# A recommender's 1,600 gather steps: the loop laid out straight, and the row weights summed into PSUM

## The chip, the cores and the metric

The kernel runs on one core of a Trainium2 chip. The metric is the device time in microseconds (us), the median of several runs. A separate execution with the hardware profiler on gives the profile; its own time is shown beside the median, because the two are not equal here.

The engines of a core are named as in the profile: PE multiplies matrices (PEld is its weight load), DVE does elementwise work and reductions, ACT activation functions, POOL (GpSimd) here issues the indirect DMAs, SP issues plain ones.

## The reference

16,384 samples, each with a history of 200 items, an item, a user and a category. Embeddings have 64 columns. What is computed, cut to what matters:

```python
def dice(x, alpha, axis):
    mean = jnp.mean(x, axis=axis, keepdims=True)
    var = jnp.var(x, axis=axis, keepdims=True)
    p = jax.nn.sigmoid((x - mean) * jax.lax.rsqrt(var + EPS))
    return x * (p + alpha * (1.0 - p))

u, it, c = u_emb[user], i_emb[item], c_emb[cate]
h = i_emb[hist]                                   # 200 x 16384 x 64
itb = jnp.broadcast_to(it[None], h.shape)
feat = jnp.concatenate([h, itb, h - itb, h * itb], axis=-1)
a = dice(feat @ au_W1 + au_b1, au_alpha, axis=1)  # 36 columns, moments over the samples
w = a @ au_W2 + au_b2                             # one weight for a history row
cur = jnp.sum(w * jax.lax.stop_gradient(h), axis=0)
z = jnp.concatenate([u, it, c, cur], axis=-1)
z = dice(z @ W1 + b1, alpha1, axis=0)
z = dice(z @ W2 + b2, alpha2, axis=0)
return z @ W3 + b3
```

Nearly all the time is in the lines from `h` to `cur`.

## The kernel before

**Prologue.** The kernel first multiplies the whole item table by the part of `au_W1` that acts on h alone, and writes a table in DRAM (`table`) whose rows are 128 numbers: the embedding (64) and this product (64 with padding). The part that depends on the item alone is written to `xi`, in 8 pieces. Users, items and categories are gathered and laid out for the head (`uicT`).

**Steps.** The history is worked off in 1,600 steps: 200 history positions (`l`) by 8 pieces (`ND`) of 2,048 samples, 16 on each of 128 partitions (`TD`). Step k does, written out in this order by `step` (from line 462), the work of several steps at once, so that a step's work is spread over eleven:

- `fetch(k)`: 16 indirect DMAs on POOL (line 213 in `gather`), each for 128 rows of 512 bytes from `table` into one of 12 `land` buffers, by indices in `idx` (SBUF); and the piece of `xi`, on SP's queue.
- `turn(k-1)`, DVE: line 390 transposes the embeddings from `land` into PSUM (`ph`); line 391 multiplies them by the item (`itT`) into `hx`; line 392 transposes the second half of the rows.
- `product(k-1)`, PE (line 244): `hx` times `blk_m` onto what ACT has put into `px` (line 476, `preload`).
- `hidden(k-2)`, DVE: line 397 adds both halves and puts the sum back into `land`; line 399 takes its statistics.
- `gates(k-10)`, ACT: lines 405 and 410, the sigmoid and its scale and shift, into `pg` (PSUM).
- `weigh(k-10)`, DVE: line 417 multiplies gate and value in `pg`; line 418 transposes back into `land`; line 420 sums each row to its weight `r`; line 425 multiplies the embedding rows by r plus a bias, into `pg`; line 429 adds that to `cur`.
- In one step of eight, `moments`: the mean and variance of a history position, some fifteen small DVE instructions and a square root on ACT (lines 436 to 460).

Here `ph` and `pg` are PSUM tiles, `px` are two PSUM tiles, and `r` is a small SBUF tile with two buffers. In the steps `ph` is written and read by DVE alone.

**Order and queues.** Each engine works through its own list in the order of the code; `tc.manual_schedule()` keeps the order as written. Semaphores carry the dependencies: a gather waits for the last use of its `land` buffer and for the gather eight places before it; line 390 waits for all 16 gathers of its step.

**The loop.** Of the 200 history positions, `rest_l` = 200 % 24 + 24 = 32 are laid out straight at the end (256 steps). The 168 before run in a hardware loop, `tc.For_i`, of 7 passes with 24 positions (192 steps) each. The body is straight code. The indices of the next position are loaded by `fetch_ids` in every eighth step, at an address that depends on the loop's register:

```python
        rest_l = L % LPB + LPB
        with tc.For_i(0, L - rest_l, LPB) as l0:
            with tc.manual_schedule():
                for k in range(LPB * ND):
                    fetch_ids(k, l0, LPB + 1)
                    step(k)
```

In the straight part `step` gets `last`, by which the final 144 steps (`SPAN`) use one of the `px` tiles only; the other one computes the first layer of the head piece by piece (`base_of_layer1`). After the steps the head follows: two layers with dice and the output.

Of the kernel before, what the change touches and what calls it, by code (L numbers as in the profile page):

```python
# [8 lines left out]
F32 = mybir.dt.float32  # L9
# [5 lines left out]
P = 128  # L15
# [2 lines left out]
CH = 512  # L18
S = 32
CD = 2 * CH  # L20
LPB = 24
LAND = 12
SPAN = 144
EARLY = 4
IDX = 2
# [4 lines left out]
def din_kernel(  # L30
# [25 lines left out]
    L, B = r_hist.shape  # L56
    NT = B // P
    TD = 2 * CD // P
    ND = NT // TD
# [5 lines left out]
    small = ctx.enter_context(tc.tile_pool(name="small", bufs=2))  # L65
# [40 lines left out]
    for a in range(P // S):  # L106
        r = ts(a, S)
# [4 lines left out]
        for q, (a0, n) in enumerate(parts):  # L112
            c, w = slice(a * S, a * S + n), au_w[r, :, :, a0 : a0 + n]
# [3 lines left out]
    for a in range(P // S):  # L117
        for q, (a0, n) in enumerate(parts):
            r, u = slice(a * S, a * S + n), slice(a0, a0 + n)
# [21 lines left out]
    ph = psum.tile([P, CD], F32, name="ph")  # L141
# [78 lines left out]
    def load_hist_ids(i, l):  # L220
        nc.sync.dma_start(idx[i], r_hist[ds(l, 1), :].rearrange("l (p n) -> p (l n)", n=NT))

    def halves(t, n=TD):

        return t.rearrange("p (e n t) -> p e n t", e=2, t=S)[:, :, :n]
# [14 lines left out]
    def first_layer(dst, blk, rhs, n=CH, onto=False):  # L240

        for q in range(2):
            for e in range(2):
                nc.tensor.matmul(  # L244
                    dst[:, q * CH : q * CH + n], blk[:, e, q], rhs[:, e * CH : e * CH + n],
                    start=(e == 0 and not onto), stop=(e == 1), skip_group_check=onto,
                )
# [101 lines left out]
    with ExitStack() as main:  # L349
# [25 lines left out]
        def by_row(t):  # L375
            return t.rearrange("p (n d) -> p n d", d=D)

        def x_of(k):
            return of_rows(land[k % LAND][:, :, D:])

        def fetch(k):
            l, c = divmod(k, ND)
            gather(land[k % LAND], idx[l % IDX][:, ts(c, TD)], table)
            nc.sync.dma_start(xit[k % XI], xi[c])

        def turn(k):

            rows = land[k % LAND]
            hm, hw = hx[k % 2][:, 0], hx[k % 2][:, 1]
            nc.vector.transpose(halves(ph), of_rows(rows[:, :, :D]))  # L390
            nc.vector.tensor_mul(hm, ph, itT[:, k % ND])  # L391
            nc.vector.transpose(halves(hw), of_rows(rows[:, :, D:]))  # L392

        def hidden(k, px):

            l, c = divmod(k, ND)
            nc.vector.tensor_add(x_of(k), halves(px), halves(hx[k % 2][:, 1]))  # L397
            for q in range(2):
                nc.vector.bn_stats(stats[l % 2][:, q, c, :], x_of(k)[:, q])  # L399
# [15 lines left out]
        def weigh(k):  # L415

            nc.vector.tensor_mul(halves(pg), halves(pg), x_of(k))  # L417
            nc.vector.transpose(x_of(k), halves(pg))  # L418
            r = small.tile([P, TD], F32, tag="r", name="r")
            nc.vector.tensor_reduce(  # L420
                r, land[k % LAND][:, :, D:], mybir.AxisListType.X, ALU.add
            )
            c = k % ND
            rows = land[k % LAND][:, :, :D]
            nc.vector.scalar_tensor_tensor(  # L425
                by_row(pg), r.unsqueeze(2).to_broadcast([P, TD, D]), au_bias2, rows,
                ALU.add, ALU.mult,
            )
            nc.vector.tensor_add(cur[:, ts(c, TD)], by_row(pg), cur[:, ts(c, TD)])  # L429
# [32 lines left out]
        def step(k, last=None):  # L462


            def has(j):
                return last is None or j <= last

            def single(j):

                return last is not None and j > last - SPAN  # L470

            def px_of(j):
                return pxs[0 if single(j) else j % 2]

            def preload(j):
                nc.scalar.copy(px_of(j), xit[j % XI])  # L476

            def product(j):
                first_layer(px_of(j), blk_m, hx[j % 2][:, 0], onto=True)

            if has(k):
                fetch(k)
            if has(k - 1):
                turn(k - 1)
                if not single(k - 1):
                    product(k - 1)
            if has(k - 10):
                if k % ND == 2:
                    moments((k - 10) // ND)
                gates(k - 10)  # L490
                weigh(k - 10)
            if has(k - 2):
                hidden(k - 2, px_of(k - 2))
            if has(k - 1) and single(k - 1):
                preload(k - 1)
                product(k - 1)
            if has(k) and not single(k):
                preload(k)

        def fetch_ids(k, l0, n):  # L500
            l, c = divmod(k, ND)
            if c == 0 and l + 1 < n:
                load_hist_ids((l + 1) % IDX, l0 + l + 1)

        def window(j):
            return slice(2 * ZB * (J - 1 - j), 2 * ZB * (J - 1 - j) + P)
# [22 lines left out]
                        yield  # L529
                        yield  # L530

        rest_l = L % LPB + LPB
        with tc.For_i(0, L - rest_l, LPB) as l0:
            with tc.manual_schedule():
                for k in range(LPB * ND):
                    fetch_ids(k, l0, LPB + 1)
                    step(k)


        K = rest_l * ND  # L540

        def home(i):
            t = land[(K + i // 2) % LAND].rearrange("p (s n) d -> p s (n d)", s=2)
            return t[:, i % 2]
# [6 lines left out]
        def rest_of(c):  # L551
            return home(homes[ND + c // J])

        def load_base(*cs):
            for c in cs:
                nc.sync.dma_start(z_of(c), zbase[c])
# [45 lines left out]
        with tc.manual_schedule():  # L602
            work = base_of_layer1()
            for k in range(K):
                fetch_ids(k, L - rest_l, rest_l)
                step(k, last=K - 1)
                if k > K - SPAN:
                    next(work, None)
            load_base(0, 1)
            for k in range(K, K + 10):  # L610
                step(k, last=K - 1)
                if k < K + 4:
                    load_base(*((2, 3), (ND, ND + 1), (4, 5), (6, 7))[k - K])
                c = k - K - 2
                if c >= 1:
                    keep1(c - 1)
                if c >= 0:
                    layer1(c)
            keep1(ND - 1)

            spare = [home(i) for i in range(18, 24)]
            fa, fb = row_factors(0, ZA, P), row_factors(1, ZB, P)
            def activated(c):
                if c % J == 0:
                    dice(rest_of(c), rest_of(c), spare[4 + c // J], fb, zb)
                a = spare[c % 4]
                dice(a, z_of(c), a, fa, za)
                layer(
                    (px, pz, pg, ph)[c % 4][: 2 * Z2], [(w2a, a), (w2b[:, c % J], rest_of(c))]
                )  # L630

            def keep2(c):
                t = home(10 + c)[: 2 * Z2]
                nc.scalar.activation(
                    t, (px, pz, pg, ph)[c % 4][: 2 * Z2], AF.Identity, bias=z2[0]
                )
                row_sums(2, 2 * Z2, c, t)

            for c in range(ND + 2):
                if c < ND:  # L640
                    activated(c)
                if c >= 2:
                    keep2(c - 2)
            f2 = row_factors(2, Z2, 2 * Z2)
            n = ND * 2 * ZO
            for c in range(ND):
                a = spare[c % 4]
                dice(a, home(10 + c)[: 2 * Z2], a, f2, z2)
                at = (ND - 1 - c) * 2 * ZO
                for i in range(2):  # L650
                    nc.tensor.matmul(  # L651
                        px[:n, ts(i, CH)], w3[:, at : at + n], a[: 2 * Z2, ts(i, CH)],
                        start=(c == 0), stop=(c == ND - 1),
                    )

            rT, res = spare[4][:S], spare[5][:S]
            nc.vector.transpose(rT, px[:S])
            rT = rT.rearrange("t (i n c g o) -> t i g c n o", i=2, n=TD, c=ND, g=2)
            for i in range(2):
                for g in range(2):  # L660
                    nc.vector.tensor_add(
                        res[:, ts(2 * i + g, NT * ZO)].rearrange("t (c n o) -> t c n o", c=ND, n=TD),
                        rT[:, i, g],
                        bias3.unsqueeze(1).unsqueeze(1).to_broadcast([S, ND, TD, ZO]),
                    )
            nc.sync.dma_start(
                out.rearrange("(q t n) o -> t q (n o)", t=S, n=NT),
                res.rearrange("t (q m) -> t q m", q=4),
            )
# [30 lines left out]
```

## Time and profile before

| | us |
|---|---|
| median of 3 runs | 36713.39 |
| lowest and highest run | 36705.22, 36721.51 |
| the profiled execution | 32925.16 |
| its span, first to last instruction | 32922.9 |
| first gather of the steps begins at | 488.6 |
| last gather of the steps begins at | 32710.6 |
| DVE idle at line 390, waiting for gathers | 10590.4 |
| ACT idle at line 476, waiting for DVE line 397 | 22124.3 |

The profiled execution is the shorter one, by about a tenth. All durations of single instructions come from it.

A line of the groups reads: source line, engine, operation, what it writes and reads, shape, count; then the busy time in all in us and the mean of one in ns; then the engine's idle time just before these instructions, and what ended it. "issue" means that the engine waited for nothing that the profile shows. A line of the timeline reads: start in us from the start of the span, duration in us, engine, line, operation, operands, count, and in brackets the idle time before it.

### The profile page before, as it was taken

The page shows a single profiled execution, that of the slowest core. Times are in us where ns is not written, and L with a number is a line of the kernel's source. Part 1 is how long each engine was busy: PE and PEld are TensorE (multiplying, and loading weights), DVE is VectorE, ACT ScalarE, POOL GpSimd, SP SyncE. Part 2 cuts the span into 40 slices and gives each one's busy share as a digit, 9 for nine tenths or more (in the row PEclk, how much of TensorE's full clock was granted, in tenths as well). Part 3 has the DMA queues.
Part 4 walks back from the last instruction along what each step waited for, and adds up shares of the span by engine and source line. Part 5 has one row for each costly group of instructions (what it writes and reads, how often), then busy time and mean ns, then how long its engine had stood idle before and what let it go on. Part 6 is the DMA issues. An engine that isn't in the chain of part 4 may idle for free. (4 is left out here: it accounts for less than half of the span.)

```text
span 32922.9 us, 106947 instructions
## 1 busy us (share of the span) xinstructions
PE 9897.1 (30%) x13650; PEld 3847.8 (12%) x13650; DVE 20486.1 (62%) x21482; ACT 7127.0 (22%) x8732; POOL 24717.0 (75%) x25991
## 2 busy tenths in 40 slices
PE   4222222222222222222222222222222222223333
PEld 1111111111111111111111111111111111111111
DVE  5666666666666666666666666666666666666666
ACT  1222222222222222222222222222222222222222
POOL 7777777777777777777777777777777777777775
PEclk7666666666666666666666666666666666666666
DMA  5222222222222222222222222222222222223332
GB/s 161 80 79 78 79 78 79 79 78 78 79 79 79 79 78 79 79 78 78 79 79 79 79 79 78 79 79 78 78 80 79 78 80 78 79 79 88 92 92 66
DMA packets 1219178, 2681.59 MB, mean 81 GB/s; under 512 B 552540, under 2 KB 578684, under 8 KB 1212284
## 3 DMA queue, kind: packets, MB, share of 16 engines
q0 software_dynamic: 831488, 1691.97, 19.6%
q1 hardware_dynamic: 375228, 914.56, 9.0%
q10 hardware_dynamic: 11712, 67.98, 0.5%
q14 instruction: 635, 5.20, 0.1%
q8 instruction: 115, 1.88, 0.0%
HBM read 2599.36 MB, written 73.35 MB: 81 GB/s over the span
## 5 line engine op out<-in xcount | busy, mean ns | idle before, releaser
L213 POOL DMA_INDIRECT land<-table,idx x25600 | 24348.1, 951 | 7875.1 <-issue 7674.0
L244 PE MATMUL px<-hx,blk_m 128*128 128x512 f32 x12824 | 9453.7, 905 | 22727.6 <-DVE hx L391 20633.8
L390 DVE STREAM_TRANSPOSE ph<-land 128x1024 f32<-128x1024 f32 x1601 | 2016.5, 1259 | 10697.6 <-DMA land<-table,idx 10590.4
L244 PEld LDWEIGHTS px<-hx,blk_m 128*128 128x128 f32 x12824 | 3670.8, 301 | 28507.3 <-issue 23397.1
L476 ACT COPY px<-xit 128x1024 f32<-128x1024 f32 x1600 | 1626.6, 1017 | 22124.3 <-DVE land L397 22124.3
L405 ACT ACTIVATE pg<-land,fac 128x512 f32<-128x512 f32 x3220 | 2508.9, 779 | 85.8 <-DVE cur L429 25.0
L417 DVE TENSOR_TENSOR pg<-pg,land 128x1024 f32<-128x1024 f32 x1610 | 1939.0, 1204 | 925.2 <-ACT pg L410 925.0
L410 ACT ACTIVATE pg<-pg,au_al,au_1al 128x512 f32<-128x512 f32 x3220 | 2419.2, 751 | 106.6
L425 DVE SCALAR_TENSOR_TENSOR pg<-r,au_bias,land 128x1024 f32<-128x1024 f32 x1610 | 2085.1, 1295 | 56.7
L399 DVE BATCH_NORM_STATS2 st<-land 128x6 f32<-128x512 f32 x3204 | 2061.9, 685 | 54.3
L418 DVE STREAM_TRANSPOSE land<-pg 128x1024 f32<-128x1024 f32 x1610 | 2011.7, 1250 | 55.4
L429 DVE TENSOR_TENSOR cur<-pg,cur 128x1024 f32<-128x1024 f32 x1610 | 1970.7, 1224 | 55.0
L420 DVE TENSOR_REDUCE r<-land 128x16 f32<-128x1024 f32 x1610 | 1964.0, 1220 | 55.3
L391 DVE TENSOR_TENSOR hx<-ph,itT 128x1024 f32<-128x1024 f32 x1601 | 1960.3, 1224 | 56.2
L392 DVE STREAM_TRANSPOSE hx<-land 128x1024 f32<-128x1024 f32 x1601 | 1975.3, 1234 | 0.0
L397 DVE TENSOR_TENSOR land<-px,hx 128x1024 f32<-128x1024 f32 x1602 | 1945.1, 1214 | 0.0
L455 ACT ACTIVATE std<-var,eps 32x2 f32<-32x2 f32 x201 | 59.2, 295 | 2577.3 <-DVE var L451 2577.3
L405 ACT ACT_TABLE_LOAD x209 | 268.1, 1283 | 297.5 <-DVE fac L460 172.0
L244 PE MATMUL px<-rT,blk_h 128*128 128x512 f32 (+1 forms) x392 | 220.9, 726 | 168.2 <-DVE rT L295 168.2
L455 ACT ACT_TABLE_LOAD x201 | 257.9, 1283 | 3.5
L439 DVE COPY every<-mv 32x4 f32<-32x4 f32 x804 | 161.7, 201 | 15.2
L213 POOL DMA_INDIRECT land<-in_L_rec_i_emb,ids x128 | 126.4, 987 | 41.0 <-issue 38.6
(110 smaller groups left out, 1537.0 us busy)
## 6 DMA issues: line engine op xcount, KB each, us to landing
xit<-xi SPq DMA_DIRECT2D x1601, 512.0 KB
land<-table,idx POOLq DMA_INDIRECT x25600
table<-tab ACTq DMA_DIRECT2D x48, 1024.0 KB
tab<-in_L_rec_i_emb SPq DMA_DIRECT2D x48, 512.0 KB
zt<-uicT SPq DMA_DIRECT2D x48, 512.0 KB
idx<-in_r_hist SPq DMA_DIRECT2D x200, 64.0 KB
uicT<-t ACTq DMA_DIRECT2D x24, 512.0 KB
zbase<-zt SPq DMA_DIRECT2D x10, 512.0 KB
```

The lines of the kernel that those rows point to most:

```text
L213: nc.gpsimd.indirect_dma_start(out=dst[:, n, :], out_offset=None, in_=rows, in_offset=bass.IndirectOffsetOnAxis(ap=ids[:, n : n + 1], axis=0),
L244: nc.tensor.matmul(dst[:, q * CH : q * CH + n], blk[:, e, q], rhs[:, e * CH : e * CH + n], start=(e == 0 and not onto), stop=(e == 1), ski ...
L390: nc.vector.transpose(halves(ph), of_rows(rows[:, :, :D]))
L391: nc.vector.tensor_mul(hm, ph, itT[:, k % ND])
L392: nc.vector.transpose(halves(hw), of_rows(rows[:, :, D:]))
L399: nc.vector.bn_stats(stats[l % 2][:, q, c, :], x_of(k)[:, q])
L405: nc.scalar.activation(halves(pg)[:, q], x_of(k)[:, q], AF.Sigmoid, bias=facs[i][:, 1, q : q + 1], scale=facs[i][:, 0, q : q + 1],)
L410: nc.scalar.activation(pg[:, ts(q, CH)], pg[:, ts(q, CH)], AF.Identity, bias=au_al[:, q : q + 1], scale=au_1al[:, q : q + 1],)
L418: nc.vector.transpose(x_of(k), halves(pg))
L420: nc.vector.tensor_reduce(r, land[k % LAND][:, :, D:], mybir.AxisListType.X, ALU.add)
L425: nc.vector.scalar_tensor_tensor(by_row(pg), r.unsqueeze(2).to_broadcast([P, TD, D]), au_bias2, rows, ALU.add, ALU.mult,)
L429: nc.vector.tensor_add(cur[:, ts(c, TD)], by_row(pg), cur[:, ts(c, TD)])
```

## The change

Three things: the hardware loop goes, and all 200 history positions are laid out straight in the part that was the tail; `fetch_ids` loses the loop's register; and `r`, the weights of the rows, is no longer a tile in SBUF, but the first 16 columns of the PSUM tile `ph`. The lines after it are moved up by one, by eight after the loop: what was line 425 is line 424.

```diff
-LPB = 24
@@ weigh
             nc.vector.tensor_mul(halves(pg), halves(pg), x_of(k))
             nc.vector.transpose(x_of(k), halves(pg))
-            r = small.tile([P, TD], F32, tag="r", name="r")
+            r = ph[:, :TD]
             nc.vector.tensor_reduce(
                 r, land[k % LAND][:, :, D:], mybir.AxisListType.X, ALU.add
             )
@@
-        def fetch_ids(k, l0, n):
+        def fetch_ids(k):
             l, c = divmod(k, ND)
-            if c == 0 and l + 1 < n:
-                load_hist_ids((l + 1) % IDX, l0 + l + 1)
+            if c == 0 and l + 1 < L:
+                load_hist_ids((l + 1) % IDX, l + 1)
@@
-        rest_l = L % LPB + LPB
-        with tc.For_i(0, L - rest_l, LPB) as l0:
-            with tc.manual_schedule():
-                for k in range(LPB * ND):
-                    fetch_ids(k, l0, LPB + 1)
-                    step(k)
-
-
-        K = rest_l * ND
+
+        K = L * ND
@@ the steps and the head
             for k in range(K):
-                fetch_ids(k, L - rest_l, rest_l)
+                fetch_ids(k)
                 step(k, last=K - 1)
```

## The prediction

> **What bounds the kernel now.** I read the page's head and busy shares first, then its costliest groups, then a stretch of the timeline inside a pass of the loop, and last a stretch across one of the loop's turns. Busy shares and groups:
>
> ```profile
> span 32922.9 us, 106947 instructions
> PE 9897.1 (30%) x13650; PEld 3847.8 (12%) x13650; DVE 20486.1 (62%) x21482; ACT 7127.0 (22%) x8732; POOL 24717.0 (75%) x25991
> L213 POOL DMA_INDIRECT land<-table,idx x25600 | 24348.1, 951 | 7875.1 <-issue 7674.0
> L390 DVE STREAM_TRANSPOSE ph<-land 128x1024 f32<-128x1024 f32 x1601 | 2016.5, 1259 | 10697.6 <-DMA land<-table,idx 10590.4
> L425 DVE SCALAR_TENSOR_TENSOR pg<-r,au_bias,land 128x1024 f32<-128x1024 f32 x1610 | 2085.1, 1295 | 56.7
> ```
>
> POOL is 75% busy, but its 25,600 gathers with the idle time between them make 24,348.1 + 7,875.1 = 32,223 us, and that idle time is "issue": POOL waits for nobody. The first gather starts at 488.6 us. With what follows the last one that is the whole span. DVE, the next engine, waits 10,590 us for gathers at L390, some 6.6 us in each of 1,600 steps. So the end is set by the pace at which POOL issues gathers, and a change is worth what it does to that pace.
>
> The pace is even. This is DVE beside POOL in an ordinary step:
>
> ```profile
> 15024.31 1.22 DVE L420 TENSOR_REDUCE r<-land 128x16 f32<-128x1024 f32 x1
> 15024.33 0.94 POOL L213 DMA_INDIRECT land<-table,idx  x1 [0.31 <-issue]
> ...
> 15025.56 1.29 DVE L425 SCALAR_TENSOR_TENSOR pg<-r,au_bias,land 128x1024 f32<-128x1024 f32 x1
> 15025.58 0.95 POOL L213 DMA_INDIRECT land<-table,idx  x1 [0.30 <-issue]
> ...
> 15026.83 0.94 POOL L213 DMA_INDIRECT land<-table,idx  x1 [0.30 <-issue]
> ```
>
> A gather takes 0.94 us, the pause 0.30, the period is 1.249 us. And this is the first step after a turn of the loop:
>
> ```profile
> 15959.49 0.94 POOL L213 DMA_INDIRECT land<-table,idx  x1 [0.30 <-issue]
> 15970.05 1.28 ACT L405 ACT_TABLE_LOAD   x1 [15.81 <-PEq L533]
> 15970.10 1.26 DVE L390 STREAM_TRANSPOSE ph<-land 128x1024 f32<-128x1024 f32 x1 [15.59 <-PEq L533]
> ...
> 15971.12 0.94 POOL L213 DMA_INDIRECT land<-table,idx  x1 [10.69 <-issue]
> ...
> 15978.35 1.29 DVE L425 SCALAR_TENSOR_TENSOR pg<-r,au_bias,land 128x1024 f32<-128x1024 f32 x1
> 15978.61 1.84 POOL L213 DMA_INDIRECT land<-table,idx  x1 [0.30 <-issue]
> 15979.68 1.22 DVE L429 TENSOR_TENSOR cur<-pg,cur 128x1024 f32<-128x1024 f32 x1
> ```
>
> Two things are to be seen. At the turn (L533) all engines stop and POOL idles 10.69 us where it idles 0.30. And the gather that begins 0.26 us after the start of L425 takes 1.84 us, not 0.94. In the ordinary step L425 began within 20 ns of a gather, so that the next one came 1.27 us later and lost nothing. L425 is the one DVE instruction of a step that reads two large operands from SBUF (r and the rows in land); L391, L397, L417 and L429 have one of theirs in PSUM. Over the trace, gathers that begin 200 to 400 ns after L425 take 1.80 us in the mean (200 of them), 600 to 800 ns after it 1.37 us, 800 to 1,000 ns after it 1.22 us; those that begin under any other DVE line, at any distance, take 0.94. The held gather always ends about 2.1 us after L425's start: it resumes some 1.16 us after that start. So L425 holds a gather for up to about 1.04 us (the longest gather is 1,981 ns, against a median of 944), and what a step loses depends on the phase of L425 against the gathers.
>
> [...] a gather reads its indices from idx in SBUF, and is held under L425 alone, by up to 1.04 us. [...]
>
> **The change part by part.** The profiled execution took 32,925.16 us, 2 us over its span; the median of the runs is 36,713.39, so 3,788 us more, 148 ns for each of 25,600 gathers. No view tells where these lie. I make the sum on the profiled execution first and then ask what carries over.
>
> *The loop goes.* 1,344 of 1,600 steps stood in 7 passes of 192. POOL's pauses at the turns: 7.42 us after the first pass, 10.69 each after the next five, 3.32 at the exit; less 0.30 each that is 62 us. All of it is POOL's time, hence on the path. The instructions of a step and their waits stay as they are, and so do both halves of the ring (192 is a multiple of 12 land buffers and of 2 index buffers). SP issues the same 200 index loads, now from constant addresses; they have a whole row of 8 steps, 160 us, to land. Does straight code cost POOL more? The last 256 steps were straight already: there the mean period is 1.256 us, as in the passes. I take nothing; an open bound is below.
>
> *r moves to ph.* L420 writes 128x16 to PSUM, L425 reads it from there. [...] ph is free then: L390 fills it and L391 empties it earlier in the same step on the same engine, so no wait is added, and PE does not touch ph in the steps. [...]
>
> L425 then has one SBUF input and should hold no gather. In the profiled execution that gives back 25,600 × (951.1 − 944) ns = 182 us; some 200 of the held gathers are those of the one step in eight that runs the moments, where DVE comes about a microsecond late against POOL, as after a turn.
>
> Sum for the profiled execution: 62 + 182 = 244 us of 32,925, or 0.7%. What is late next is still POOL, at 25,600 × 1.249.
>
> *What carries over.* The loss at L425 hangs on a phase that 35 ns decide: the ordinary step runs free only because L425's start falls on a gather's start. In the runs without a profile a gather's period is another: 36,713 − 489 − 211 (the prologue and the tail) = 36,013 us over 25,600, or 1.407 us in the mean if POOL's pace carries it all. The chain from the last landing to L425 (some 8 us) then falls elsewhere in the period. Bounds for a step's loss: nothing, if the phase is lucky, and 1.04 us, so 0 to 1,664 us in all. With no reason for any one phase I take the mean over a period of 1.407: a gather is held in 1.04/1.407 = 74% of phases, by 0.52 us on average, 0.385 us a step, 616 us in all. With 62 us for the loop: 36,713 − 678 = 36,035.
>
> **The rivals.** *The phase in the runs is the profile's.* For it: the phase follows from DVE lengths near the gather's period, which hold in both. Against: the runs are 11% slower, so some length differs. 36,713 − 244 = 36,469.
>
> *Nothing measurable comes of it.* If the runs' phase is lucky in all steps, the loop's 62 us alone are left: 36,651, within 0.2% (73 us, about what a measurement of this kernel can tell from no change).
>
> *The unexplained 3,788 us belong to the loop form or to L425 in a way that the profile does not show.* Without them: 32,925 − 244 = 32,681. For it: held gathers are the only loss on POOL that hangs on timing. Against: one L425 in a step can hold one gather, 1.04 us, and the excess is 2.37 us a step.
>
> *Slower: straight code feeds POOL more slowly than the loop.* [...] the runs have an excess whose place is unknown. Its place would be the pause of 0.30 us before each of the 21,504 gathers that were in the loop. It decides from 678/21,504 = 32 ns each (11 ns against the profile's 244). At 5% of 1.407 us, 70 ns, it costs 1,505 us: 36,713 − 244 + 1,505 = 37,974. Against it: the equal periods in the straight part of the profile[...].
>
> **How the numbers follow.** Uniform phase 0.45; the profile's phase 0.28; nothing measurable 0.10; the large gain 0.05; slower 0.12. The forecast is that of the first, 36,035. Its own range is 34,990 (1,664 + 62 gained) to 36,640. Widened to 34,980 to 36,700 it takes in the first three cases, some 0.83. Faster by over 0.2%: 0.45 + 0.28 + 0.05 = 0.78; the same 0.10; slower 0.12.
>
> **What would show it.** In the profile after: the longest gather of the steps near 950 ns, not 1,981, and their mean duration at 944; no pause of POOL above a few us once the first steps are through; gathers' busy and idle time together near 31,980 us; the span near 32,680; L424 (today's L425) still 1.29 us. If gathers are still held near 1.8 us, the two-input reading is wrong. If the gather's period is above 1.26 us, straight code has a price. If the runs gain far more or less than the profile, the phase, or the unexplained excess, decided.

## The result, and the profile after

| | before, us | after, us | ratio, 95% interval |
|---|---|---|---|
| first comparison, 12 runs each | 36717.45 | 36711.88 | 0.9998, 0.999 to 1.0006 |
| predicted | | 36035 | 0.9815 |

The change does nothing that can be measured. These are the lines of the page of the kernel after that answer to those shown of before:

```profile
span 36719.1 us, 106470 instructions
PE 9930.6 (27%) x13650; PEld 3856.1 (11%) x13650; DVE 20623.6 (56%) x21482; ACT 7114.3 (19%) x8725; POOL 27140.0 (74%) x25991
L212 POOL DMA_INDIRECT land<-table,idx x25600 | 26771.0, 1046 | 9142.2 <-issue 8927.5
L396 DVE TENSOR_TENSOR land<-px,hx 128x1024 f32<-128x1024 f32 x1602 | 1959.8, 1223 | 8263.6 <-remote 5280.2
L389 DVE STREAM_TRANSPOSE ph<-land 128x1024 f32<-128x1024 f32 x1601 | 2012.6, 1257 | 5571.7 <-DMA land<-table,idx 5298.4
L424 DVE SCALAR_TENSOR_TENSOR pg<-ph,au_bias,land 128x1024 f32<-128x1024 f32 x1610 | 2081.7, 1293 | 57.2
```

This profile has the span of the timed runs; that of before had been 10% shorter. The gathers with their pauses make 26,771.0 + 9,142.2 = 35,913 us, 1.403 us for each, where the first profile had 32,223 us and 1.259. A gather's mean is 1,046 ns, not the 944 of the forecast, although L424 no longer reads two operands from SBUF. New is a wait of DVE at L396, 5,280 us in all, for PE's semaphore ("remote": its release has no record); the wait for gathers at L389 is smaller by about the same.

The timeline of the kernel after shows how the gathers come to that mean. It is 15 us in the middle of the run:

```profile
15002.42 1.12 POOL L212 DMA_INDIRECT land<-table,idx  x1 [0.30 <-issue]
...
15003.84 0.94 POOL L212 DMA_INDIRECT land<-table,idx  x1 [0.30 <-issue]
15003.98 1.29 DVE L424 SCALAR_TENSOR_TENSOR pg<-ph,au_bias,land 128x1024 f32<-128x1024 f32 x1
...
15005.09 0.94 POOL L212 DMA_INDIRECT land<-table,idx  x1 [0.30 <-issue]
...
15013.83 0.94 POOL L212 DMA_INDIRECT land<-table,idx  x1 [0.30 <-issue]
...
15015.60 1.93 POOL L212 DMA_INDIRECT land<-table,idx  x1 [0.83 <-issue]
...
15017.84 1.13 POOL L212 DMA_INDIRECT land<-table,idx  x1 [0.30 <-issue]
...
15019.27 1.09 POOL L212 DMA_INDIRECT land<-table,idx  x1 [0.31 <-issue]
```

From 15,003.84 to 15,013.83 there are eight periods of 1.249 us: POOL's own pace, as in the first profile. L424 holds nothing here: over the whole trace gathers that begin 200 to 400 ns after it take 0.99 us in the mean (179 of them, my count), where L425 had made them 1.80. Then a gather takes 1.93 us after a pause of 0.83, and the next ones come some 1.4 us apart. POOL runs ahead, is held, and runs ahead again. Counted over the whole trace, 16 gathers take 22.43 us in the mean, 1.402 us each.

### The profile page after: what moved, and what is told of

The parts are those of the page before. It is cut to its first block, busy times and chain, and to the rows that moved or that the text cites. A ratio compares the mean times of both kernels' runs of the same rounds, so it can differ in the third digit from the quotient of the medians.

```text
span 36719.1 us, 106470 instructions
## 1 busy us (share of the span) xinstructions
PE 9930.6 (27%) x13650; PEld 3856.1 (11%) x13650; DVE 20623.6 (56%) x21482; ACT 7114.3 (19%) x8725; POOL 27140.0 (74%) x25991
## 3 DMA queue, kind: packets, MB, share of 16 engines
q0 software_dynamic: 831488, 1691.97, 17.8%
q8 instruction: 112, 1.84, 0.0%
## 5 line engine op out<-in xcount | busy, mean ns | idle before, releaser
L212 POOL DMA_INDIRECT land<-table,idx x25600 | 26771.0, 1046 | 9142.2 <-issue 8927.5
L396 DVE TENSOR_TENSOR land<-px,hx 128x1024 f32<-128x1024 f32 x1602 | 1959.8, 1223 | 8263.6 <-remote 5280.2
L389 DVE STREAM_TRANSPOSE ph<-land 128x1024 f32<-128x1024 f32 x1601 | 2012.6, 1257 | 5571.7 <-DMA land<-table,idx 5298.4
L424 DVE SCALAR_TENSOR_TENSOR pg<-ph,au_bias,land 128x1024 f32<-128x1024 f32 x1610 | 2081.7, 1293 | 57.2
L419 DVE TENSOR_REDUCE ph<-land 128x16 f32<-128x1024 f32 x1610 | 1976.9, 1228 | 55.5
L459 DVE COPY fac<-fac 32x4 f32<-32x4 f32 x603 | 125.5, 208 | 385.7 <-issue 365.7
```

What stands on the lines that cost most here:

```text
L212: nc.gpsimd.indirect_dma_start(out=dst[:, n, :], out_offset=None, in_=rows, in_offset=bass.IndirectOffsetOnAxis(ap=ids[:, n : n + 1], axis=0),
L419: nc.vector.tensor_reduce(r, land[k % LAND][:, :, D:], mybir.AxisListType.X, ALU.add)
L424: nc.vector.scalar_tensor_tensor(by_row(pg), r.unsqueeze(2).to_broadcast([P, TD, D]), au_bias2, rows, ALU.add, ALU.mult,)
```

## The experiments

One number orders them: the time of the kernel before on the same chip. On four chips (0, 7, 8 and 14 in the record) it was 36.69 to 36.78 ms, on one (2) it was 32,979 us. The chip of the first profile and of the first comparison is not on record.

**Another pace, a loop that is quick when profiled, or two edits that cancel?** The kernel before once more; the loop kept, with r in PSUM; and straight code, with r in SBUF. The edit of the second to the kernel before, and of the third to the kernel after:

```diff
-            r = small.tile([P, TD], F32, tag="r", name="r")
+            r = ph[:, :TD]
```
```diff
-            r = ph[:, :TD]
+            r = small.tile([P, TD], F32, tag="r", name="r")
```

> The kernel before, unchanged, profiled once more. Theory A (the quick profile of before was one execution in another pace, of 20.0 us a step, which the runs never have): this profile now shows 22.4 us a step and a span near 36,710 us, with late matmul semaphores and gathers of 1.05 us in the mean, as the profile after. Theory B (the loop form is quick whenever it is profiled, and slow in the runs): the profile is near 32,925 us again while the timed run is near 36,715. Theory C (two edits of opposite sign cancel) says nothing of this run but a timed run near 36,715.

> The loop stays, only r moves to PSUM. Theory A: no change in the runs, 36,650 to 36,720 us, since L425's hold of a gather is not what sets the slow pace. Theory C: r in PSUM gives back up to 0.5 us a step, so 35,900 to 36,500, and the straight form then costs as much.

> Laid out straight, r stays in SBUF. Theory A: no change in the runs, 36,640 to 36,720 us. Theory C: the straight form costs what r in PSUM gives, 36,900 to 37,500; and the profile shows gathers held under the line that reads r.

Measured beside the kernel before, at 36,689.42 us on that chip:

| | us | ratio, 95% interval |
|---|---|---|
| before again | 36681.59 | 0.9998, 0.9989 to 1.0007 |
| loop, r in PSUM | 36685.51 | 0.9996, 0.9988 to 1.0005 |
| straight, r in SBUF | 36669.84 | 0.9992, 0.9983 to 1.0001 |

All four forms take the same time, in the profiled execution as in the others, so nothing cancels, and the loop isn't quick when profiled: this profile of the kernel before has a span of 36,671.4 us. The first one had been taken at another pace. Both losses that the prediction priced are still there in it. The timeline across a turn of the loop, kernel before again:

```profile
9191.98 0.94 POOL L213 DMA_INDIRECT land<-table,idx  x1 [0.30 <-issue]
9216.80 1.26 DVE L390 STREAM_TRANSPOSE ph<-land 128x1024 f32<-128x1024 f32 x1 [32.40 <-PEq L533]
9217.82 0.94 POOL L213 DMA_INDIRECT land<-table,idx  x1 [24.90 <-issue]
...
9225.04 1.29 DVE L425 SCALAR_TENSOR_TENSOR pg<-r,au_bias,land 128x1024 f32<-128x1024 f32 x1
9225.31 1.84 POOL L213 DMA_INDIRECT land<-table,idx  x1 [0.30 <-issue]
```

POOL loses 24.90 us at the turn, more than the 10.69 of the first profile, and L425 stretches a gather to 1.84 us as it did there. Yet from 50 gathers before a turn to 300 after it the mean period is 1,398.5 ns (my count over the records): right after the pause some hundred gathers come 1.27 us apart, until the lost time is made up. A pause of POOL is absorbed.

So are the held gathers. In this profile 1,470 gathers begin within 1.16 us after the start of an L425, and take 1,536 ns in the mean; in that of the loop with r in PSUM it is 1,473 gathers and 1,024 ns (my counts). Some 750 us of POOL are given back, and the two kernels take 36,681.59 and 36,685.51 us.

**What of a step sets 1.400 us?** Four kernels take parts out of the kernel after: the load of the piece of xi; the matrix product; everything in a step but the gathers and that load; and the gathers.

```diff
+        nc.sync.dma_start(xit[0], xi[0])
@@ fetch
-            nc.sync.dma_start(xit[k % XI], xi[c])
```
```diff
-                first_layer(px_of(j), blk_m, hx[j % 2][:, 0], onto=True)
+                pass
```
```diff
             if has(k):
                 fetch(k)
+            return
```
```diff
-            gather(land[k % LAND], idx[l % IDX][:, ts(c, TD)], table)
+            if k < LAND:
+                gather(land[k % LAND], idx[l % IDX][:, ts(c, TD)], table)
```

> The kernel after without the load of the item's part (512 KB of xi) in each step; its two buffers are loaded once, so that the first-layer sums are those of fixed pieces. In the profile after, the longest gather of a step (1.9 us) and the 0.15 us longer ones around it stand beside and after that load. If the load is the cause, the step falls to 16 x 1.249 = 20.0 us and the time to about 32,700 us. If it only stands near by chance, the time stays within 1% of 36,710.

> The kernel after without TensorE's product in the steps (the item term is left out of the first layer). All profiles since the first show POOL at 1.400 us a gather and TensorE's semaphore 5 to 14 us behind its last matmul. Theory P (TensorE's work or its late semaphore slows the step): the gather falls to 1.249 us and the time to about 32,700 us. Theory S (POOL's gathers have a pace of 1.400 us of their own, from something behind POOL that the profile doesn't show): the time stays within 1% of 36,700 us.

> Of a step only the gathers and the load of the item's part are left; DVE, ACT and TensorE do nothing in the steps. Theory S: 25,600 gathers at 1.400 us, about 36,400 us in all. Theory P, or any theory in which an engine beside POOL slows it: 1.249 us a gather, about 32,500 us.

> The gathers are left out after the first twelve steps; all else of a step stays, on the rows that lie in the buffers. DVE is then the bound by its busy time, about 12.4 us a step and 15 with its waits: 20,000 to 25,000 us if TensorE is on time. If TensorE's semaphore is late by itself, 5 to 14 us a product, the step stays near 20 us and the time above 30,000; if it is late only because of the gathers, the lag in this profile is near nothing, as in the first profile of before (0.015 us).

Measured: without the load 36,663.42 us (ratio 0.9993, 0.9986 to 1.0); without the product 36,629.13 in one run, the gathers alone 36,511.69 in one run, without gathers 22,199.74 in one run; before beside these three 36,704.3. Neither the xi transfers nor the work of TensorE, DVE and ACT slows POOL. Gathers alone take 99.5% of the time, and their timeline is even:

```profile
15001.65 1.09 POOL L212 DMA_INDIRECT land<-table,idx  x1 [0.31 <-issue]
15003.05 1.09 POOL L212 DMA_INDIRECT land<-table,idx  x1 [0.30 <-issue]
15004.45 1.09 POOL L212 DMA_INDIRECT land<-table,idx  x1 [0.30 <-issue]
```

1.40 us from one start to the next, and 25,600 × 1.400 = 35,840 us. The median period is 1,400 ns; over blocks of 256 gathers the mean lies between 1,398 and 1,402 ns (my count). Once in 128 gathers a few come up to 0.7 us late, and the next ones, at 1.25 us, make it up. The first 180 gathers of the steps or so still came at 1.249 us; what changes after them is not shown. Without gathers, the page shows DVE as the next bound, with 22,198 us to the span:

```profile
span 22198.0 us, 65740 instructions
PE 9921.0 (45%) x13650; PEld 3852.5 (17%) x13650; DVE 20300.8 (91%) x21482; ACT 7118.0 (32%) x8725; POOL 549.9 (2%) x583
```

**Is it POOL's own pace, or one behind it?** If POOL itself needs 1.400 us for a gather, more work on POOL costs its full length. If the pace is imposed from behind, POOL has 16 × (1.400 − 1.249) = 2.4 us a step to spare. Five or sixteen small memsets on a tile of their own go behind the gathers of each step of the kernel after. Two more kernels change the size of a gather, with the gathers alone: half the rows, or half the bytes of a row (`[:64]` in the index and the target, or `i_emb` in place of `table`).

```diff
             nc.sync.dma_start(xit[k % XI], xi[c])
+            for _ in range(5):
+                nc.gpsimd.memset(pad, 0.0)
```
```diff
-            gather(land[k % LAND], idx[l % IDX][:, ts(c, TD)], table)
+            for n in range(TD):
+                nc.gpsimd.indirect_dma_start(
+                    out=land[k % LAND][:64, n, :],
+                    out_offset=None,
+                    in_=table,
+                    in_offset=bass.IndirectOffsetOnAxis(
+                        ap=idx[l % IDX][:64, c * TD + n : c * TD + n + 1], axis=0
+                    ),
+                )
```
```diff
-            gather(land[k % LAND], idx[l % IDX][:, ts(c, TD)], table)
+            gather(land[k % LAND][:, :, :D], idx[l % IDX][:, ts(c, TD)], i_emb)
```

> The kernel after, with five small POOL memsets (128x192 f32, on a tile of their own) after the 16 gathers of each step; nothing else changes. Small POOL instructions take 0.1 to 0.33 us in the trace of the kernel after, so with pauses I expect 1.0 to 1.8 us of POOL a step. Theory Q (a gather's 1.400 us is imposed behind POOL, whose own pace is 1.249 us, so a step has 16 x 0.151 = 2.4 us of POOL to spare): no change, 36,700 within 60. Theory P (POOL itself needs 1.400 us for a gather): 1,600 to 2,900 us more, 38,300 to 39,600. If Q holds, the mean period from the first gather of one step to that of the next stays 22.40 us.

> As the run with five memsets, but with sixteen a step: 3.2 to 5.8 us of POOL. Theory Q: the first 2.4 us are free, the rest is paid: 1,600 x (0.8 to 3.4) = 1,300 to 5,400 us more, and the difference between the POOL time added and the time paid is 2.4 us a step. Theory P: all of it is paid, 5,100 to 9,300 us more.

> Gathers alone (the steps do nothing else but load xi), each gather for 64 rows of 512 bytes instead of 128. Left out: all of a step's arithmetic and half its rows. If the pace of 1.400 us belongs to the gather as such: 36,510 as with 128 rows. If it belongs to rows or bytes: it falls to 0.70 us, and POOL's own pace decides, 1.249 us or less, so 32,700 at most, and 18,700 if POOL's own pace too goes with the rows.

> Gathers alone, each gather for 128 rows of 256 bytes (from the item table itself) instead of 512. Left out: all of a step's arithmetic and half the bytes of each row. If the pace of 1.400 us belongs to the gather or to its rows: 36,510. If it belongs to the bytes moved: POOL's own pace decides, 1.249 us, and 32,700.

By chance these four ran on a chip on which the kernel before takes 32,979.46 us, in all of 7 runs within 5 us. Measured there: five memsets 35,535.77 us (ratio 1.0775, 1.0757 to 1.0793), sixteen 41,086.56 (1.2458, 1.2437 to 1.2479), half the rows 31,442.38, half the bytes 32,579.67. Taken by its letter, theory Q missed: nothing was free. But its premise, the 1.400 us, was missing on this chip. The groups of the kernel with five memsets:

```profile
L212 POOL DMA_INDIRECT land<-table,idx x25600 | 24166.2, 944 | 8147.3 <-issue 8121.1
L386 POOL MEMSET pad<- 128x192 f32 x8000 | 2091.5, 261 | 368.1
```

No gather is held here: the mean is 944 ns, as forecast for r in PSUM, and the longest of the steps takes 961 ns (my count), against 1,981 in the first profile of before. 32,979 us is near what that first profile showed (32,925). So the same kernels meet two paces, and where it is the quick one, POOL sets the end. All runs of one visit to a chip had the same pace; whether the pace belongs to the chip or to a state that it was in is not shown, since no chip was met at both.

**The same kernel where the pace is 1.400 us.** The kernel after, the two single edits and the five memsets went to a chip again; then the kernel after twice more, once with the gathers of 64 rows.

> The kernel after, unchanged, beside the kernel before on the same chip. Theory Q (each chip has its own pace for a stream of gathers; where it is 1.400 us, POOL's gains are absorbed, where it is quick, POOL's own pace of 1.249 us sets the end and they count). If the kernel before takes 36,700 on this chip: the same time, within 60. If it takes 32,980: 62 for the loop and up to 182 for the gathers that L425 held, 150 to 300 less, about 32,740. Theory N (the change does nothing to POOL anywhere): the same as before on either chip.

> The loop kept, r in PSUM. On a chip where the kernel before takes 32,980: theory Q expects 90 to 230 less, the held gathers alone; where it takes 36,700, no change.

> Laid out straight, r kept in SBUF. On a chip where the kernel before takes 32,980: theory Q expects about 60 less for the turns of the loop, more or less by what L425's phase against the gathers becomes; where it takes 36,700, no change.

> The five memsets a step once more; in the first run of this kernel they stood for 1.3 us of POOL work a step, on a chip where the kernel before took 32,979, and the time was 35,536. If this chip's kernel before takes 36,700: theory Q expects no change, 36,700 within 60, since 2.4 us of POOL a step are free there; theory P (POOL itself needs 1.400 us for a gather) expects 1,600 to 2,600 more. If it takes 32,980: 35,540 again.

> The kernel after, unchanged, beside the kernel before on one chip. Theory Q: where the kernel before takes 32,980, about 32,740 (62 for the loop, up to 182 for held gathers); where it takes 36,700, the same time. Theory N (the change does nothing to POOL anywhere): the same time on either chip.

> The kernel after, unchanged, beside the kernel before on one chip. Theory Q: where the kernel before takes 32,980, about 32,740 (62 for the loop, up to 182 for held gathers); where it takes 36,700, the same time. Theory N (the change does nothing to POOL anywhere): the same time on either chip.

> Gathers alone, 64 rows each; left out as before: all arithmetic of a step and half its rows. Where the kernel before takes 32,980 it took 31,400 and should again. Where it takes 36,700: 36,510, as with 128 rows, if the pace of 1.400 us belongs to the gather as such; 31,400, POOL's own pace, if it goes with rows or bytes.

All of these met chips of the longer time:

| | us | before beside it | ratio, 95% interval |
|---|---|---|---|
| after | 36673.59 | 36693.29 | 0.9995, 0.9987 to 1.0004 |
| loop, r in PSUM | 36678.6 | 36693.29 | 0.9997, 0.9988 to 1.0005 |
| straight, r in SBUF | 36667.88 | 36693.29 | 0.9992, 0.9984 to 1.0001 |
| after, five memsets a step | 36659.66 | 36693.29 | 0.9993, 0.9984 to 1.0001 |
| after, third time | 36784.2 | 36782.32 | 1.0003, 0.9994 to 1.0011 |
| after, fourth time | 36708.66 | 36721.16 | 0.9999, 0.999 to 1.0008 |
| gathers of 64 rows alone, one run | 36514.18 | 36721.16 | |

The fourth line decides. The kernel that costs 2,556 us over the kernel before on the quick chip costs nothing here. Its groups, and POOL's timeline where a step ends:

```profile
L212 POOL DMA_INDIRECT land<-table,idx x25600 | 24226.5, 946 | 8174.5 <-issue 8131.5
L386 POOL MEMSET pad<- 128x192 f32 x8000 | 2096.8, 262 | 1403.1 <-POOL pad L386 576.1
L399 DVE TENSOR_TENSOR land<-px,hx 128x1024 f32<-128x1024 f32 x1602 | 1946.7, 1215 | 0.0
```

```profile
2744.31 0.94 POOL L212 DMA_INDIRECT land<-table,idx  x1 [0.30 <-issue]
2745.24 0.28 POOL L386 MEMSET pad<- 128x192 f32 x1
2747.14 0.26 POOL L386 MEMSET pad<- 128x192 f32 x1 [1.62 <-remote]
2748.54 0.26 POOL L386 MEMSET pad<- 128x192 f32 x1 [1.14 <-issue]
2749.94 0.26 POOL L386 MEMSET pad<- 128x192 f32 x1 [1.14 <-POOL pad L386]
2751.34 0.26 POOL L386 MEMSET pad<- 128x192 f32 x1 [1.14 <-POOL pad L386]
2752.13 0.95 POOL L212 DMA_INDIRECT land<-table,idx  x1 [0.53 <-DVE pg L419]
2753.38 0.94 POOL L212 DMA_INDIRECT land<-table,idx  x1 [0.30 <-issue]
```

The gathers now take 946 ns, like on the quick chip: POOL works at its own pace, and has so little left that it is held only now and then, here at the memsets. Their pauses grow from 368 us to 1,403 us, which is most of the 1,124 us between the two chips. Gathers and memsets together make 32,401 + 3,500 = 35,901 us, within 0.1% of the gathers alone in the kernel after (35,913). The time stays, its contents change: that is a pace set from behind. What is shown to be free is the price of the five memsets on the quick chip, 1.7 us a step with their pauses and the longer wait of the gather behind them; the sixteen were not run here.

The memsets also show that more than gathers is held. The last four in the lines above start 1.40 us apart. Of 6,400 such spacings in this profile, 384 are 1.40 us and 197 are 0.70 us, within 0.02 us; on the quick chip all 6,400 are below 0.40 (my count). The memsets add no packets to the DMA queue of the gathers (831,488 with them and without), and 576.1 us of their 1,403.1 us of idle time end with the memset before.

The 64 rows test what the pace goes with. The same kernel on the quick chip, then here:

```profile
15001.05 0.89 POOL L383 DMA_INDIRECT land<-table,idx  x1 [0.30 <-issue]
15002.25 0.90 POOL L383 DMA_INDIRECT land<-table,idx  x1 [0.30 <-issue]
```

```profile
15000.66 1.10 POOL L383 DMA_INDIRECT land<-table,idx  x1 [0.30 <-issue]
15002.06 1.10 POOL L383 DMA_INDIRECT land<-table,idx  x1 [0.30 <-issue]
```

Half the rows and bytes: still 1.400 us. The pace goes with neither rows nor bytes (36,511.69 us with 128 rows, 36,514.18 with 64); what a gather of either size has in common was not varied. Slower transfers are not the cause: with the packets of the gathers' queue (831,488 for 25,984 gathers of 128 rows) counted off in order, 32 to a gather, the last one ends 2.19 us after the gather's start in the first profile of before and 2.25 us after it in the second, at the longer pace (medians, my count).

## Why the prediction was wrong

**The step that failed** is the one from the profile to the runs: "the end is set by the pace at which POOL issues gathers, and a change is worth what it does to that pace", with the runs' 1.407 us read as POOL's own period. On the chips of the runs POOL's own period is 1.249 us, as the stretches in the timeline of the kernel after show, and 1.400 us is imposed on the stream of gathers from behind POOL. The prediction had the excess in hand, 148 ns for each gather, and took it for a longer period of POOL's. It was the bound itself: (1.400 − 1.249) × 25,600 = 3,866 us, against the 3,788 us it called unexplained. By this difference 2.4 us of POOL in every step are free there, an estimate of which the five memsets show 1.7; the held gathers, at most 1.04 us a step, lie within that, and the turns of the loop are made up over the steps that follow.

**The bound in the profile** was read rightly for its pace: where gathers come 1.249 us apart POOL sets the end, and on the quick chip five memsets cost what they take.

**The loop, 62 us.** The pauses are real, even longer on the chips of the runs, and are made up within a few hundred gathers. Straight and loop code take the same time on two chips. The rival that feared a price for straight code is not borne out: the eight periods in the kernel after are 1.249 us, and so is the median period of the kernel with five memsets on the quick chip, straight code too. Both forms also load about the same bytes of instructions by their pages (queues q14 and q8), 7.08 MB with the loop and 6.81 MB without.

**r in PSUM, 182 us.** The reading of the trace was right: with one SBUF operand in that line, no gather is held under it (944 ns in the mean, 25,600 × (951.1 − 944.0) = 182 us on the quick chip). The cost on DVE is small: L419 takes 1,228 ns, against 1,220, and L424 1,293, against 1,295. Even the size of the hold in the runs was near: the 750 us counted above are 0.47 us a step, against the 0.385 expected. What was wrong is that this comes to the end in the runs. In the straight kernel with r in SBUF, gathers that begin 200 to 400 ns after that line take 1,790 ns in the mean (my count), and it is no slower.

**The rivals.** "Nothing measurable" came true, but not by its lucky phase. "The unexplained excess belongs to the loop form or to L425" is refuted by the kernels with one edit each. The listed sign "if the gather's period is above 1.26 us, straight code has a price" would have misled: the kernel with the loop has the same period.

**Not tried:** the kernel after on the quick chip; it met none. From the trace of the five memsets there an estimate can be made: 35,466 us for the profiled execution, less 2,460 for the memsets with their pauses, less 272 because the gather behind them waits 0.47 us, not 0.30, less 53 for 30 pauses of 2.08 us that only the kernels with memsets have: 32,681. With the median of the runs, 35,536, it is 32,751. Before took 32,979, so most of the prediction's 244 us may well be there; that is argued, not shown.

## What to carry to other kernels

When the profiled execution and the timed runs differ by a tenth, divide the difference by the count of the most frequent instruction before anything else, and ask whether it is a floor: here the even excess, 148 ns for each gather, was a bound of its own, and work below it was free (36,659.66 us with five memsets a step, 36,693.29 before). An engine that seems busy can be a held one: here POOL's hold stood in longer gathers (1,046 ns in the mean, not 944) and in no wait with a name. Add work to it, and see whether the time moves. On the chips of the longer time one would try fewer gathers, not quicker ones; no run here did.

## What was not expected of the hardware

- One kernel met two paces: a stream of indirect DMAs from POOL ran at 1.249 us each on one chip, and at 1.400 us in the mean on four others. Rows don't matter at the longer pace (1.400 us with 128 or 64); POOL's own period is 1.25 us for 128 rows, of 512 or of 256 bytes, and 1.205 for 64.
- Where gathers are held, PE's semaphores are late too: in the kernel after, L396 starts 7.1 us behind the end of the last matmul (the median of the 1,372 steps in which it waits, my count); with no gathers, or in the first profile, PE's semaphore comes 0.015 us behind it. With the memsets, which leave POOL hardly ahead, the wait at L399 is 0.0. Late semaphores would also account for memsets that wait for each other; that is argued.
- What holds them stays open. The records of semaphore updates differ with the pace: with half the rows, on the quick chip there are about 17 for each gather (449,718 in all), on the others 53,886 for the same kernel, one in 0.700 us, thus two for each gather of 1.400 us; in the first profiles of before and after it is 477,634 and 54,910 (my counts). But with five memsets a step the records come one in 0.302 us, at the same pace of gathers, so the two don't simply go together. Every timed run here has a span and a granted clock on record too, so none is known to have been made without records, and whether the pace is a price of the recording can't be told.
